# Four PSUM banks for the picks of a graph layer, with a pair's sums moved into the bank of the position row

## The chip, the cores and the metric

The kernel runs on one core of a Trainium2 chip. The metric is the device time of one execution in microseconds (us). The core has TensorE (PE; its weight loads are listed apart as PEld), VectorE (DVE), ScalarE (ACT), GpSimd (POOL) and SyncE (SP, which here only issues DMAs). TensorE writes its products to PSUM, eight banks of 512 32-bit numbers in each of 128 partitions; DVE and ACT read and write PSUM too. Each engine works through its own queue in order, and engines wait for each other through semaphores.

## The reference: what is computed

One message-passing layer on a graph of 6250 nodes and 100000 edges, feature width 128. The edges are sorted by `dst`.

```python
edge_index = jnp.stack([src, dst])          # row = src, col = dst
msg_in = jnp.concatenate([x[row], x[col], edge_attr], axis=-1)
h = msg_in @ W + b                          # (100000, 384) @ (384, 128)
h = (h - mean(h)) * rsqrt(var(h) + 1e-5) * gamma + beta
msg = relu(h)
out = segment_sum(msg, row, num_segments=6250)
x = layernorm(x + out)
```

## The kernel before, in words

The product with `W` is split in three. The part of `x[col]` comes from a table of projected nodes: edges are sorted by `dst`, so the rows that 512 edges need lie in a window of 42 nodes, and a one-hot matrix picks them. The part of the edge's own features is a plain product. Both are added in PSUM for a group of four tiles of 128 edges. There are 782 tiles, 196 such groups, called q. In `edges` TensorE makes them (lines 619 and 623, tile `hp`), in `evict` ACT copies them out (line 633), and in `scatters` POOL writes every row by an indirect DMA to the place in memory that belongs to the block of its `src` (line 650).

That place is computed by `places`, in 20 pieces of 12 to 44 tiles. 50 blocks of 125 nodes hold the sources. A piece makes a one-hot array of blocks by tiles (DVE, line 451, which compares with the position row), scans it for running counts (line 455, which reads a zero beside that row), sums counts over partitions with two small matmuls (lines 467 and 468), adds them to what is already taken (lines 470 to 472), multiplies (line 474), and adds the resulting terms over the 50 blocks (line 502): `PG` blocks side by side in PSUM per matmul, all matmuls adding to the same columns, and DVE adds the `PG` parts in the end (line 507). The pieces are spread over the edge groups by `steps_at`: eleven steps a piece.

The edges are cut in six splits (`SPLITS`). When the rows of one split have arrived, they are loaded back, two blocks at a time: a pair holds eight tiles of rows in splits 0 to 2, six in split 3, four in splits 4 and 5. 25 pairs make a split. The `Pair` class works on the first five splits while later edges are still made; `Unit` works on the last split, in the tail. For a pair:

- `ones`: DVE compares each row's position in its block with the position row (line 742) and so makes one-hot tiles;
- `turn`, `turned`: TensorE transposes them (line 754, bank `tr`), ACT copies them out (line 758);
- `seed`: ACT copies the edge rows into a PSUM bank named `sel` (line 764), up to four tiles to a bank;
- `pick`: TensorE adds to it the rows of `x[row]`'s projection (line 781);
- `square`, `root`, `scale`: ACT sums the squares (lines 790 and 793), DVE makes the reciprocal and scales and clips (lines 799 and 805), which frees the bank;
- `sums`: TensorE adds the messages of each node (line 814, into bank `pa`);
- `add`: DVE adds that to the running total (line 819).

In `Unit` the same steps stand at lines 847 (`ones`), 866 and 872 (`pick`), 883 (`square`), 898 (`scale`), 912 (`sums`, every other one into `pa`, the rest into `hp`) and 918 (`add`); lines 925 to 961 finish the layer norm, and line 930 reads a row of `beta` from the columns of the counts.

The order on PE, DVE, ACT and SP is written out by hand. `work` goes through steps; a pair starts one every four steps, and `FLOW` gives how many steps after its start each part of it is issued:

```python
FLOW = [(14, second(lambda x: x.add())), (11, second(lambda x: (x.root(1), x.scale(1)))),
        (13, single(lambda x: x.add())),
        (9, lambda x: (x.root(0), x.scale(0))), (13, second(lambda x: x.sums())),
        ...
        (10, single(lambda x: x.sums())),
        (0, lambda x: x.ones()),
```

`second` is for pairs with two groups of tiles (eight or six), `single` for pairs of four. So `ones` of pair p+3 is issued at step 12 of pair p, its `sums` at step 13 and its `add` at step 14; for pairs of four `sums` come at step 10, `ones` of pair p+3 at 12 and `add` at 13. `steps_due` ties steps to edge groups. POOL's scatters from group 13 on are tied to TensorE instructions as well, to be spread evenly.

The eight banks are: two `hp`, three `sel`, one `tr`, one `pa`, and one, `beside_t`, with the position row (128 32-bit numbers, `iota_p`), a zero (`zero_p`), 50 numbers of `places` (`at`) and, from column 192, the `counts`. `project`, which makes the tables of projected nodes at the beginning, borrows `sel` and `tr` in turn (lines 391 to 417).

Of the kernel before, what the change touches and what calls it, by code (L numbers as in the profile page):

```python
# [8 lines left out]
F32 = mybir.dt.float32  # L9
BF16 = mybir.dt.bfloat16  # L10
# [6 lines left out]
P = 128  # L17
D = 128
# [6 lines left out]
NB, BN = 50, 125  # L25
# [6 lines left out]
PIECES = 196  # L32
TABLE_FROM = [0, 13, 45, PIECES]
HALF = PIECES // 2
BANKS = {"hp": 2, "sel": 3, "tr": 1}


SPLITS = [(168, 4, 320, [12, 24, 44, 44, 44]),
# [7 lines left out]
BY_PE = 4  # L46
FN = 4

PG = 7
PG_AT = 192  # L50
XG = 4
ROW = 132
ACW = 130
# [13 lines left out]
def dram_ap(t, offset, ap):  # L67
    return bass.AP(tensor=t.tensor, offset=t.offset + offset, ap=ap)
# [7 lines left out]
def row_bc(t, n):  # L76

    return t.unsqueeze(1).to_broadcast([t.shape[0], n, t.shape[1]])


def flat(t):
    return t.rearrange("p t d -> p (t d)")


def fast_path(ctx, tc, io, bad_d, found):
# [3 lines left out]
    nc = tc.nc  # L89
    first_tile = first_tiles()  # L90
    const = ctx.enter_context(tc.tile_pool(name="const", bufs=1))
    dram = ctx.enter_context(tc.tile_pool(name="dram", bufs=1, space=bass.MemoryType.DRAM))
    psum = ctx.enter_context(tc.tile_pool(name="psum", bufs=1, space=bass.MemoryType.PSUM))
# [5 lines left out]
    def pe(i, cost=1):  # L99
        done.append((i.ins, cost))  # L100
        return i
# [72 lines left out]
    iota_i = const.tile([P, P], I32, name="iota_i")  # L174
# [9 lines left out]
    iota_row = const.tile([P, P], F32, name="iota_row")  # L184

    beside_t = psum.tile([P, 512], F32, name="beside")
    beside, counts = beside_t[:, :PG_AT], beside_t[:, PG_AT:]
    iota_p, zero_p, at = beside[:, 0:P], beside[:, P:P + 1], beside[:, P + 8:P + 8 + NB]
    part = const.tile([P, 1], F32, name="part")
    before = const.tile([P, P], BF16, name="before")  # L190
    ident_h = const.tile([P, P], BF16, name="ident_h")
# [7 lines left out]
    over_w = const.tile([P, 2], F32, name="over_w")  # L199

    def constants():
        nc.vector.tensor_copy(iota_p, iota_i)
        nc.vector.tensor_copy(iota_row, iota_i)
        nc.vector.tensor_copy(part, part_i)
        nc.vector.memset(zero_p, 0.0)
        nc.vector.tensor_scalar(over_w[:, 0:1], part, WN - 0.5, float(WN), op0=ALU.is_gt,
                                op1=ALU.mult)
        nc.vector.tensor_scalar(over_w[:, 1:2], part, 2 * WN - 0.5, float(WN), op0=ALU.is_gt,
                                op1=ALU.mult)
        nc.vector.tensor_scalar(before, iota_row, part, None, op0=ALU.is_gt)  # L210
        nc.vector.tensor_tensor(part_w, part, over_w[:, 0:1], op=ALU.subtract)
        nc.vector.tensor_tensor(part_w, part_w, over_w[:, 1:2], op=ALU.subtract)
        nc.vector.tensor_copy(ident_h, ident)
        nc.vector.tensor_scalar(minus_h, ident, -1.0, None, op0=ALU.mult)
# [36 lines left out]
    def signs():  # L251
        nc.vector.tensor_scalar(gamma_r, gamma_r, 0.0, 2.0, op0=ALU.is_ge, op1=ALU.mult)
        nc.vector.tensor_scalar(sgn_r, gamma_r, -1.0, None, op0=ALU.add)
        spread = psum.tile([P, 512], F32, name="pa")[:, :D]
        nc.tensor.matmul(spread, ones_h[0:1, :], sgn_r, start=True, stop=True)
        nc.scalar.copy(sgn, spread)

# [115 lines left out]
    n_banks = 0  # L373

    def store_part(xb_t, i):
        nc.sync.dma_start(dram_ap(xb_d[0], i * TABLES[0][1] * D, [[XG * D, P], [1, XG * D]]),
                          flat(xb_t[:, i]))

    def project(g, k):

        nonlocal n_banks
        t0 = g * XG
        m = XG if k == 1 else min(XG, NB - t0)
        xT = xT_of[g, k % 2]
        name = ("sel", "sel", "tr", "sel")[n_banks % 4]
        n_banks += 1
        ps = psum.tile([P, XG, P], F32, name=name, bufs=BANKS[name])
        for j in range(m):  # L390
            nc.tensor.matmul(ps[:, j, :], xT[:, j * P:(j + 1) * P], w[:, min(k, 1), :],
                             start=j == 0, stop=j == m - 1, skip_group_check=True)
        yield
        full = ps[:, :m, :]
        if k == 0:
            o = [xa[:, t0:t0 + m, i * D:(i + 1) * D] for i in range(3)]
            nc.vector.tensor_tensor(full, full, row_bc(bias, m), op=ALU.add)
            yield
        else:
            xb_t = proj_pool.tile([P, 3, XG, D], BF16, name="xb", bufs=4)  # L400
            o = [xb_t[:, i, :m, :] for i in range(3)]
        for i in range(2):
            nc.scalar.copy(o[i], full)
            if g == 0 and k == 1:
                store_part(xb_t, i)
            yield
            nc.tensor.matmul(full, minus_h, o[i], start=False, stop=True, skip_group_check=True)
            yield
        if g == 0 and k == 1:
            nc.scalar.copy(o[2], full)  # L410
            store_part(xb_t, 2)
            yield
            nc.sync.dma_start(
                dram_ap(xb_d[1], 0, [[XG * D, P], [TABLES[1][1] * D, 3], [1, XG * D]]),
                xb_t.rearrange("p i t d -> p i (t d)"))
            return
        nc.vector.tensor_copy(o[2], full)
        yield
        if k == 1:
            n0 = g * XG * P  # L420
            for (lo, hi), t in zip(TABLES[:2], xb_d):
                if lo <= n0 < hi:
                    nc.sync.dma_start(
                        dram_ap(t, (n0 - lo) * D, [[XG * D, P], [(hi - lo) * D, 3], [1, XG * D]]),
                        xb_t.rearrange("p i t d -> p i (t d)"))
        if k == 2:
            nc.sync.dma_start(
                dram_ap(xb_d[2], t0 * D, [[NB * D, P], [NPAD * D, 3], [1, m * D]]),
                xb_t[:, :, :m, :].rearrange("p i t d -> p i (t d)"))
        yield  # L430
# [7 lines left out]
    def places(s, t0, T):  # L438
# [49 lines left out]
        else:  # L488
# [7 lines left out]
            for k, (wt, v, back) in enumerate(terms):  # L496
                for b in range(0, NB, PG):
                    c0, c1 = b * T, min(b + PG, NB) * T
                    skip = back if b == 0 else 0
# [3 lines left out]
                                     start=(k == 0 and b == 0),  # L503
                                     stop=(k == len(terms) - 1 and b + PG >= NB),
                                     skip_group_check=True)
            yield
            nc.vector.tensor_reduce(pos, sums[:, :PG * T].rearrange("p (g t) -> p t g", g=PG),
                                    axis=AX.X, op=ALU.add)
# [88 lines left out]
    def edge_hot(q):  # L597
# [5 lines left out]
        if q < BY_PE:  # L603
            db = psum.tile([P, PT * P], F32, name="sel", bufs=BANKS["sel"])
            nc.tensor.matmul(db, ones_h[0:1, :], drel0[0:1, q, :], start=True, stop=True)
# [60 lines left out]
    def open_late():  # L666
# [8 lines left out]

        for _ in range(BANKS["sel"]):
            sel = psum.tile([P, PT, P], F32, name="sel", bufs=BANKS["sel"])
            nc.tensor.matmul(flat(sel), ones_h, row_bc(ones_h, PT), start=True, stop=True)
# [29 lines left out]
    def acc_scale(i0, i1):  # L708
        if i0 == 0:
            nc.vector.memset(acc[:, :, D:ACW], 0.0)  # L710
            late["rg"] = psum.tile([P, PT, P], F32, name="sel", bufs=BANKS["sel"])[:, 0, :]
            nc.vector.tensor_copy(late["rg"], rg)
# [15 lines left out]
    class Pair:  # L728
# [17 lines left out]
        def turn(self):  # L746
# [3 lines left out]
            for j0, m in [(0, self.k)]:  # L750
                tr = psum.tile([P, PT, P], F32, name="tr", bufs=BANKS["tr"]).bitcast(BF16)
                tr = tr.rearrange("p t (h d) -> p (t h) d", h=2)
# [54 lines left out]

        def sums(self):
            k = self.k
            pa_t = psum.tile([P, 512], F32, name="pa")  # L810
            self.pa = pa_t[:, :2 * ACW].rearrange("p (h d) -> p h d", h=2)
            for h in range(2):
                for j in range(h, k, 2):
                    pe(nc.tensor.matmul(self.pa[:, h, :], self.ohe[:, j, :], self.msg[:, j, :],  # L814
                                        start=(j == h), stop=(j == k - 2 + h)), 4)
# [12 lines left out]
    class Unit:  # L828
# [73 lines left out]
        def sums(self, g):  # L902
            if (self.p0 + g) % 2:
                pa_t = psum.tile([P, PT, P], F32, name="hp", bufs=BANKS["hp"])
                pa = flat(pa_t)
            else:
                pa = psum.tile([P, 512], F32, name="pa")
            pa = pa[:, :2 * ACW].rearrange("p (h d) -> p h d", h=2)
            for h in range(2):
                for j in range(h, self.kp, 2):  # L910
                    jj = g * self.kp + j
                    nc.tensor.matmul(pa[:, h, :], self.ohe[:, jj, :], self.msg[:, jj, :],
                                     start=(j == h), stop=(j == self.kp - 2 + h))
            self.pa = {**getattr(self, "pa", {}), g: pa}
# [75 lines left out]

    warm_up(6)
    constants()
    signs()
    warm_up(4)
    source_blocks(0, n0, 0)
# [244 lines left out]
    a, b, c, d = units[-4:]  # L1240
# [272 lines left out]
```

## Time and profile before

| | |
|---|---|
| median of 3 runs | 1356.2 us (1353.18 to 1357.1) |
| profiled execution | 1355.95 us, span 1354.1 us |
| mean TensorE clock granted | 0.855 of full speed |
| busy PE, PEld | 978.5, 869.8 us |
| busy DVE, ACT, POOL | 852.2, 766.6, 799.0 us |
| instructions | 27281 |
| mean DMA rate | 183 GB/s |

A group row of the profile names line, engine and operation, what is written and read with its shape, and how often; then the busy time in us, the mean of one in ns, and the idle time of the engine just before, with whoever ended it. "issue" means that the engine waited for nothing the profile shows, "remote" that the source is not told. A row of waits gives who waited for whom, the total in us, how often, and the longest. A timeline row gives start and length in us; consecutive instructions of one kind are merged. Matmuls overlap: a burst's pace is read from the start of one row to the start of the next. An fp32 product counts as two matmuls.

### The profile page before, as it was taken

What the parts mean: (1) busy time and instruction counts of PE and PEld (TensorE: products, weight loads), DVE (VectorE), ACT (ScalarE), POOL (GpSimd) and SP (SyncE); (2) the same over time, 40 slices, a digit from 0 to 9 for tenths busy, and PEclk for the clock granted to TensorE, in tenths of its full rate; (3) what the DMA queues carried; (4) which work ended last, traced back from release to release, by engine and by line L of the source; (5) the groups of instructions that cost most, each with busy time, mean ns of one, the idle gap of its engine ahead of it and who ended that gap; (6) DMA issues with size and microseconds to landing.
All of it is one profiled execution on the core that took longest, in us unless ns stands there. A gap on an engine that the chain in (4) does not pass through costs nothing. (4 is left out here: it accounts for less than half of the span.)

```text
span 1354.1 us, 27281 instructions
## 1 busy us (share of the span) xinstructions
PE 978.5 (72%) x8886; PEld 869.8 (64%) x8886; DVE 852.2 (63%) x2376; ACT 766.6 (57%) x2988; POOL 799.0 (59%) x830
## 2 busy tenths in 40 slices
PE   7555546365768777777877778778878787776895
PEld 5454535344757766676666767777778787665674
DVE  8572425514665666656575667678688877654797
ACT  4223322112656655565555567677779788755796
POOL 3656666666666665666566666656665556556054
PEclk9768687666888887888888798989999999988998
DMA  7857677445666654556756555666667655543332
GB/s 225 251 172 243 191 229 223 138 155 167 192 204 208 203 160 162 166 181 193 219 177 195 174 191 180 218 199 191 188 200 235 189 186 188 158 147 99 108 126 70
DMA packets 128050, 247.20 MB, mean 183 GB/s; under 512 B 47005, under 2 KB 61231, under 8 KB 127897
## 3 DMA queue, kind: packets, MB, share of 16 engines
q1 hardware_dynamic: 101924, 191.92, 46.8%
q0 software_dynamic: 25104, 53.05, 11.1%
q8 instruction: 71, 1.16, 0.4%
q14 instruction: 81, 0.66, 0.1%
q10 hardware_dynamic: 870, 0.40, 0.1%
HBM read 155.49 MB, written 89.80 MB: 181 GB/s over the span
## 5 line engine op out<-in xcount | busy, mean ns | idle before, releaser
L650 POOL DMA_INDIRECT sorted<-hs,place_i x782 | 760.6, 973 | 474.7 <-issue 179.7
L781 PE MATMUL sel<-xa,ohn 128*128 128x128 bf16 x2550 | 210.8, 232 | 134.7 <-issue 65.5
L790 ACT ACTIVATE sq<-sel 128x128 f32<-128x128 f32 x850 | 224.5, 281 | 140.4 <-remote 47.2
L619 PE MATMUL hp<-w,eT 128*128 128x128 f32 x1564 | 261.2, 316 | 32.4 <-issue 20.5
L814 PE MATMUL pa<-msg,ohe 128*128 128x130 f32 x1700 | 259.0, 307 | 30.0 <-DVE msg L805 14.9
L619 PEld LDWEIGHTS hp<-w,eT 128*128 128x128 f32 x1564 | 235.0, 226 | 67.2 <-issue 32.9
L781 PEld LDWEIGHTS <-ohn 128*128 128x128 bf16 x2550 | 175.0, 104 | 154.4 <-issue 136.1
L633 ACT COPY hs<-hp 128x512 f32<-128x512 f32 x196 | 114.2, 584 | 273.9 <-remote 98.5
L814 PEld LDWEIGHTS pa<-msg,ohe 128*128 128x128 f32 x1700 | 234.8, 216 | 41.5 <-issue 24.2
L805 DVE SCALAR_TENSOR_TENSOR msg<-sel,rstd,cut 128x128 f32<-128x128 f32 x850 | 240.7, 346 | 8.0
L790 ACT ACTIVATION_READ_ACCUMULATOR sq<-sel 128x1 f32 x850 | 179.8, 212 | 0.0
L819 DVE TENSOR_TENSOR acc<-acc,pa 128x260 f32<-128x260 f32 x125 | 52.9, 423 | 184.7 <-remote 72.8
L742 DVE TENSOR_TENSOR ohe<-hl,beside 128x1024 f32<-128x1024 f32 (+2 forms) x125 | 131.6, 1053 | 24.2 <-remote 7.6
L758 ACT COPY ohn<-tr 128x1024 bf16<-128x1024 bf16 (+2 forms) x125 | 109.6, 877 | 42.8 <-remote 19.2
L764 ACT COPY sel<-hl 128x512 f32<-128x512 f32 (+1 forms) x225 | 128.5, 571 | 2.0 <-DVE msg L805 2.0
L607 DVE TENSOR_SCALAR ohd<-db,part_w 128x512 bf16<-128x512 bf16 x192 | 68.6, 357 | 68.4 <-remote 36.8
L623 PE MATMUL hp<-win,ohd 126*128 126x128 bf16 x782 | 90.5, 238 | 15.9 <-issue 13.3
L799 DVE RECIPROCAL rstd<-std 128x4 f32<-128x4 f32 (+1 forms) x225 | 38.7, 172 | 90.3 <-ACT std L793 45.2
L754 PE MATMUL tr<-ident_h,ohe 128*128 128x128 bf16 x850 | 77.0, 229 | 21.9 <-issue 19.9
L623 PEld LDWEIGHTS <-ohd 126*128 126x128 bf16 x782 | 69.5, 109 | 23.3 <-issue 18.9
L754 PEld LDWEIGHTS <-ohe 128*128 128x128 bf16 x850 | 57.7, 103 | 29.9 <-issue 29.9
L793 ACT ACTIVATE std<-ss,eps 128x4 f32<-128x4 f32 (+1 forms) x225 | 67.1, 298 | 7.3
(198 smaller groups left out, 1018.9 us busy)
## 6 DMA issues: line engine op xcount, KB each, us to landing
eT<-in_eT SPq DMA_DIRECT2D x96, 512.0 KB
hl<-sorted SPq DMA_DIRECT2D x75, 528.0 KB
db<-drel_d SPq DMA_DIRECT2D x96, 256.0 KB
sorted<-empty SPq DMA_DIRECT2D x100, 198.0 KB
hl<-sorted SPq DMA_DIRECT2D x50, 264.0 KB
sorted<-hs,place_i POOLq DMA_INDIRECT x782
hl<-sorted SPq DMA_DIRECT2D x25, 396.0 KB
sorted<-empty SPq DMA_DIRECT2D x50, 132.0 KB
```

Of the source, the lines that this page charges most:

```text
L619: pe(nc.tensor.matmul(hp[:, j, :], eT[:, at], w[:, 2, :], start=j == 0, stop=False, skip_group_check=True), 4)
L623: pe(nc.tensor.matmul(hp[:, j, :], oh[:3 * WN, at], win[:3 * WN, :], start=False, stop=j == m - 1, skip_group_check=True))
L633: nc.scalar.copy(hs[:, :m, 0:D], hp[:, :m, :])
L650: i = nc.gpsimd.indirect_dma_start(out=sorted_d[s][:, :], out_offset=bass.IndirectOffsetOnAxis(ap=place_i[:parts, t:t + 1], axis=0), in_=h ...
L742: nc.vector.tensor_tensor(self.ohe[:, :k, :], self.hl[:, :k, D:D + 1].to_broadcast([P, k, P]), row_bc(iota_p, k), op=ALU.is_equal)
L754: pe(nc.tensor.transpose(tr[:, j, :], half[:, j0 + j, 1::2], ident_h))
L758: nc.scalar.copy(self.ohn[:, :self.k, :], self.tr[:, :self.k, :])
L764: nc.scalar.copy(self.sel[g][:, :m, :], self.hl[:, j0:j0 + m, 0:D])
L781: pe(nc.tensor.matmul(sel[:, j, :], self.ohn[:, j0 + j, :], xa[:, b, i * D:(i + 1) * D], start=False, stop=j == m - 1 and i == 2, skip_gro ...
L790: nc.scalar.activation(sq[:, j, :], self.sel[g][:, j, :], AF.Square, accum_out=ss[:, j:j + 1])
L805: nc.vector.scalar_tensor_tensor(self.msg[:, j0 + j, 0:D], self.sel[g][:, j, :], rstd[:, j:j + 1], cut, op0=ALU.mult, op1=ALU.max)
L814: pe(nc.tensor.matmul(self.pa[:, h, :], self.ohe[:, j, :], self.msg[:, j, :], start=(j == h), stop=(j == k - 2 + h)), 4)
```

## The change

`sel` gets a fourth bank. The bank `pa` is given up for it, and the sums of a pair (260 columns) move into `beside_t`. To make room there, the position row is kept as 128 16-bit numbers in 64 columns, and the counts get 132 columns in place of 320, so `PG` is 3 in place of 7. `project` goes through five banks in turn in place of four.

```diff
-BANKS = {"hp": 2, "sel": 3, "tr": 1}
+BANKS = {"hp": 2, "sel": 4, "tr": 1}
...
-PG = 7
-PG_AT = 192
+PG = 3
+PG_AT = 120
+PA_AT = 252
...
     beside_t = psum.tile([P, 512], F32, name="beside")
-    beside, counts = beside_t[:, :PG_AT], beside_t[:, PG_AT:]
-    iota_p, zero_p, at = beside[:, 0:P], beside[:, P:P + 1], beside[:, P + 8:P + 8 + NB]
+    counts, sums_p = beside_t[:, PG_AT:PA_AT], beside_t[:, PA_AT:]
+    iota_w, zero_p, at = beside_t[:, 0:P // 2], beside_t[:, P // 2:P // 2 + 1], beside_t[:, 68:68 + NB]
+    iota_p = iota_w.bitcast(BF16)
+    iota_h = const.tile([P, P], BF16, name="iota_h")
...
     def constants():
-        nc.vector.tensor_copy(iota_p, iota_i)
+        nc.vector.tensor_copy(iota_h, iota_i)
+        nc.vector.tensor_copy(iota_w, iota_h.bitcast(F32))
...
     def signs():
...
-        spread = psum.tile([P, 512], F32, name="pa")[:, :D]
+        spread = sums_p[:, :D]
...
-        name = ("sel", "sel", "tr", "sel")[n_banks % 4]
+        name = ("sel", "sel", "tr", "sel", "sel")[n_banks % 5]
...
         def sums(self):
             k = self.k
-            pa_t = psum.tile([P, 512], F32, name="pa")
-            self.pa = pa_t[:, :2 * ACW].rearrange("p (h d) -> p h d", h=2)
+            self.pa = sums_p.rearrange("p (h d) -> p h d", h=2)
...
             else:
-                pa = psum.tile([P, 512], F32, name="pa")
+                pa = sums_p
             pa = pa[:, :2 * ACW].rearrange("p (h d) -> p h d", h=2)
```

## The prediction

> **What bounds the kernel now.** I read the page first, then busy time by stage, then what TensorE (PE) waited for.
>
> ```profile
> span 1354.1 us, 27281 instructions
> PE 978.5 (72%) x8886; PEld 869.8 (64%) x8886; DVE 852.2 (63%) x2376; ACT 766.6 (57%) x2988; POOL 799.0 (59%) x830
> ...
> 345.00:1008.00 663.00, 512.05 (x4912) 465.09 (x4912) 432.91 (x1151) 412.07 (x1621) 409.87 (x422) 0.88 0.61 191
> 1038.00:1107.00 69.00, 57.05 (x632) 54.58 (x630) 55.62 (x160) 57.67 (x242) 39.96 (x42) 0.95 0.59 187
> 1164.00:1244.00 80.00, 59.12 (x575) 54.70 (x576) 44.37 (x139) 50.27 (x214) 43.69 (x46) 0.89 0.44 133
> 1272.00:1354.00 82.00, 67.25 (x624) 51.07 (x622) 71.19 (x289) 64.87 (x332) 36.30 (x35) 0.94 0.29 98
> ```
>
> A stage row gives the stretch, its length, busy us of PE, PEld, DVE, ACT and POOL, then TensorE's clock. The longest stage, 345 to 1008 us, holds pairs of eight tiles; 1038 to 1107 pairs of six; 1164 to 1244 pairs of four; the tail follows. No engine is full, so TensorE's idle time in the long stage must tell who sets the pace:
>
> ```profile
> PE sel L781 <- issue: 52.6, 78, 2.8
> PE sel L781 <- ACT sel L764: 22.7, 19, 3.2
> PE tr L754 <- issue: 16.7, 23, 1.2
> PE beside L502 <- issue: 13.2, 21, 1.2
> PE pa L814 <- issue: 12.7, 24, 1.2
> PE sel L781 <- ACT sc L477: 8.2, 5, 2.4
> PE hp L623 <- issue: 7.3, 13, 1.3
> PE hp L619 <- issue: 5.7, 15, 0.6
> ```
>
> The "issue" rows add to 108.2 us: TensorE stood and waited for nothing the profile shows. With 512 us of work that is 620 of 663 us; the rest is waits for other engines, mostly the two ACT rows here. So TensorE's queue sets the pace, and a new wait in it costs time unless it falls where the queue would have stood anyway. In the tail DVE is fullest (71.19 of 82).
>
> **The change, part by part.**
>
> *A fourth bank for picks.* A bank is taken by ACT's seed copy, which must wait until DVE's scale has freed it.
>
> ```profile
> L764 ACT COPY sel<-hl 128x512 f32<-128x512 f32 (+1 forms) x225 | 128.5, 571 | 2.0 <-DVE msg L805 2.0
> L391 PE MATMUL sel<-w,xT 128*128 128x128 f32 x168 | 30.6, 333 | 4.9 <-issue 3.9 <-DVE oh L451 1.0
> L866 PE MATMUL sel<-hl,ident 128*128 128x512 f32 x38 | 20.0, 608 | 0.0
> ```
>
> All 225 seeds together waited 2.0 us for a bank. The projection, which now rotates over five banks, not four, waited 1.0 us for DVE; the tail's picks waited for nothing. That picks wait for seeds (22.7 us above) comes from ACT's written order, which stays. So a gain of 0 to 3 us; I take 2.
>
> *Narrower position sums (PG 7 to 3).* Of 20 pieces of the placement the first has no such sums, the second two terms, the other 18 three. A term covers its 50 blocks in 17 matmuls, not 8: (18 × 3 + 2) × 9 = 504 more matmuls, each with a weight load, over the same columns.
>
> ```profile
> 733.72 1.01 PE L502 MATMUL beside<-far,twice_f 128*128 128x280 f16 x8
> 734.58 2.03 PE L814 MATMUL pa<-msg,ohe 128*128 128x130 f32 x16
> 738.73 0.83 PE L781 MATMUL sel<-xa,ohn 128*128 128x128 bf16 x12
> 739.40 1.11 PE L619 MATMUL hp<-w,eT 128*128 128x128 f32 x8
> ...
> L502 PEld LDWEIGHTS <-ident_f 128*128 128x128 f16 x160 | 17.1, 111 | 31.0 <-issue 25.9
> ...
> PE beside L502 <- issue: 15.7, 24, 1.2
> ```
>
> From start to start, eight of these matmuls took 0.86 us for 50 × 40 = 2000 columns, 0.43 ns a column; twelve picks of 128 columns took 0.67 us, 56 ns each, of which 55 are columns. So short matmuls with a load each add about 1 ns: 0.5 us in all. At the other end each load overlaps nothing: 504 × 0.111 = 56 us. The picks are the nearest row, so I take 2 us; more matmuls on the same columns cannot gain. Standing for issue came to 15.7 us over the 448 such matmuls of now, 35 ns each; if it goes by count the new ones bring 504 × 0.035 = 18 us, if by time nothing. I take 4, since the stalls are uneven and no row ties them to the count.
>
> The DVE reduction that reads them shrinks:
>
> ```profile
> L507 DVE TENSOR_REDUCE pos<-beside 128x44 f32<-128x308 f32 x3 | 1.4, 473 | 9.2 <-remote 9.2
> L507 DVE TENSOR_REDUCE pos<-beside 128x39 f32<-128x273 f32 x2 | 0.9, 438 | 0.0
> ```
>
> 35 elements are 35 ns, so 168 fewer (of 294) save 0.17 us, 18 times: 3.0 us of DVE, hidden in DVE's idle third; at most 3 us of gain. I take none.
>
> *The position row in 16 bits.* One more cast at the start, of the sort that takes 0.2 us, ahead of a DVE wait:
>
> ```profile
> 1.35 0.28 DVE L202 CAST beside<-iota_i 128x128 f32<-128x128 int32 x1
> 3.92 0.21 DVE L252 TENSOR_SCALAR gamma_r<-gamma_r 1x128 f32<-1x128 f32 x1 [1.14 <-DMA gamma_r<-in_gamma]
> ```
>
> The 1.14 us wait for gamma hides it: nothing. The comparisons that read the row keep their element counts; what a faster rate would bring is a rival below.
>
> *A pair's sums move into the bank of that row.* This is the part that counts. The row is read by DVE's one-hot comparison (line 742) 125 times; the same bank serves nearly every DVE step of the placement. Does sharing cost a wait?
>
> ```profile
> L742 DVE TENSOR_TENSOR ohe<-hl,beside 128x1024 f32<-128x1024 f32 (+2 forms) x125 | 131.6, 1053 | 24.2 <-remote 7.6 <-PE beside L502 6.0 <-PE pa L814 5.7
> L502 PE MATMUL beside<-sc,ident_f 128*128 128x294 f16 (+7 forms) x152 | 25.2, 314 | 4.2 <-issue 3.6 <-DVE ohe L742 0.6
> L814 PE MATMUL pa<-msg,ohe 128*128 128x130 f32 x1700 | 259.0, 307 | 30.0 <-DVE msg L805 14.9 <-issue 14.6
> ```
>
> The comparison reads only the row, L502 writes only the counts beside it, other columns; still the one waited 6.0 us for the other and the other 0.6 us for the one. So columns do not matter, the bank or tile does. The sums (L814) wait for no such reader now; afterwards each must wait for the last DVE step on the bank that the program puts ahead of it, and DVE's next step on it must wait until the sums are done. Behind held sums stand the next edge products, picks and transposes in TensorE's queue; ACT's evictions and copies, and through them POOL's scatters, wait for those. [...]
>
> For the size I put the program's order beside the trace: the comparison of pair p+3 stands one step ahead of the sums of pair p. In 66 of 125 pairs the sums began before the last DVE step on the bank ahead of them had ended; the first and the last of these are
>
> ```profile
> 384.33 1.19 DVE L742 TENSOR_TENSOR ohe<-hl,beside 128x1024 f32<-128x1024 f32 x1
> 385.03 2.00 PE L814 MATMUL pa<-msg,ohe 128*128 128x130 f32 x16
> ...
> 1160.64 0.68 DVE L742 TENSOR_TENSOR ohe<-hl,beside 128x512 f32<-128x512 f32 x1
> 1159.79 1.89 PE L814 MATMUL pa<-msg,ohe 128*128 128x130 f32 x12
> ```
>
> which would wait 0.5 and 1.5 us; the 66 add to 102 us. That is the upper end, paid only if no wait shortens the next. The lower end is 0: a sum held once comes later against DVE, so the next finds the bank free. Between them:
>
> ```profile
> 345.00:1008.00 663.00, 42.68 (x284) 0.00 (x0) 195.52 (x176) 0.88 0.61 191
> 1038.00:1107.00 69.00, 2.94 (x26) 0.00 (x0) 22.31 (x24) 0.95 0.59 187
> ...
> L455 DVE TENSOR_TENSOR_SCAN sc<-oh,sc,beside 128x1050 f16<-128x1050 bf16 x8 | 19.2, 2394 | 0.0
> ```
>
> The first two rows count work on this bank alone (PE, PEld, DVE): DVE holds it 29% and 32% of the time. Sums that arrive at a random moment find it held so often, with half of a step of 1.2 us (comparison) to 2.4 us (scan) left, say 0.8 us: 0.30 × 0.8 = 0.24 us, for 100 pairs 24 us. Half of it should fall on issue stalls or waits for ACT. I take 10 us: nearer to 0 than to 102, since DVE is a third idle and can run ahead.
>
> DVE waits in turn: in 45 places its next step on the bank began before the sums ended, 49 us together, 22 of them comparisons in the pairs of four tiles. There all engines have slack (44.37 of 80 for DVE), so I price it at 0, with 0.68 us × 25 = 17 us if each comparison lands on the chain from sums to add to scale. In the tail every other sum uses the bank, behind a comparison of 1.2 us that runs during the sums ahead of it: nothing, 2 us at most.
>
> **Sum.** −2 + 2 + 4 + 10 = +14 us against the profiled execution's own 1355.95 us (the median is 1356.2, the span 1354.1): 1370 us.
>
> **The rivals.**
>
> *Each wait is paid in full.* If TensorE and DVE stay in step, a held sum delays the square, scale and comparison behind it and the next is held again: 1356 + 102 + 4 = 1462 us, or half of that excess, 1409. For it: 620 of 663 us of TensorE's queue are taken. Against: DVE's idle third.
>
> *The waits are absorbed.* Every held sum falls where TensorE would have stood (108 us of issue in the long stage): 1356 − 2 + 2 = 1356 us, no change. That waits go by columns after all (1360 us) belongs here; the 6.0 us speak against it.
>
> *Faster: the one-hot comparison of the placement doubles its rate.* With row and keys both in 16 bits, line 451 might run like line 480:
>
> ```profile
> L451 DVE TENSOR_TENSOR oh<-bkt_h,beside 128x1200 bf16<-128x1200 bf16 x1 | 1.4, 1394 | 0.0
> L480 DVE TENSOR_TENSOR sc<-sc,oh 128x1200 f16<-128x1200 f16 x1 | 0.8, 776 | 0.0
> ```
>
> That halves 38 steps, 38 × 0.55 = 21 us of DVE. It turns into time only if DVE holds TensorE: with a quarter of it, 2 for the seeds and 3 for the reduction, 1356 − 10 = 1346 us. It decides from the point where sums wait less than 5 us in all. Against: the row is read with one element repeated over all tiles of a block, which line 480 does not do. [...]
>
> *Weight loads bare.* If the loads do not overlap in these bursts, 56 + 18 + 10 us: 1440 us.
>
> **How the numbers follow.** Chances: forecast 0.52 (its own range 1360 to 1390), absorbed 0.20, faster 0.10, waits in full or half 0.12, bare loads 0.06. A measurement of this kernel can tell about 0.3%, 4 us, from no change. Faster: the rival and a little of the absorbed case, 0.12. Same: 0.19, most of the absorbed case and the forecast's foot. Slower: the rest, 0.69. The range leaves out the faster rival's better half and what lies past half-paid waits: 1351 to 1405 us.
>
> **What would show it.** Seeds (L764) no longer wait for DVE. L502 counts 952, L507 shrinks to about 0.29 us; L451 stays near 1.24 us. The sums (L814) get idle time put down to line 742, 451, 455 or 474, some 20 us or more in total, and comparisons get idle time from L814 in the pairs of four tiles. TensorE's issue total grows little. Wrong would be: sums without such waits (columns decide), waits over 60 us that all stay in the span, or a term of L502 far longer than the 0.86 us that one takes now.

## The result and the profile after

The changed kernel took 1414.57 us (median of 6 runs, 1410.46 to 1423.76) where the kernel before took 1357.29 us: 1.0442 times as long, 95% interval 1.0418 to 1.0465. That is 57 us more; 14 more were predicted. The direction was right, the size was not, and the time lies above the range (1351 to 1405 us).

First the page of the changed kernel and its busy time by stage (stretch, length, busy us of PE, PEld, DVE, ACT, POOL, TensorE's clock, DMA share, GB/s). The stages hold the same work as those shown of before: pairs of eight, six and four tiles, then the tail.

```profile
span 1408.7 us, 28285 instructions
PE 980.3 (70%) x9391; PEld 892.9 (63%) x9391; DVE 851.1 (60%) x2377; ACT 765.7 (54%) x2988; POOL 796.1 (57%) x830
...
353.00:1043.00 690.00, 505.89 (x5179) 475.94 (x5177) 432.99 (x1153) 411.39 (x1622) 407.00 (x421) 0.88 0.59 183
1073.00:1148.00 75.00, 56.74 (x617) 53.60 (x618) 53.33 (x153) 55.05 (x230) 37.73 (x40) 0.93 0.54 168
1209.00:1290.00 81.00, 61.79 (x578) 55.95 (x578) 44.18 (x137) 49.72 (x212) 45.19 (x48) 0.89 0.43 133
1319.00:1409.00 90.00, 69.03 (x624) 52.50 (x622) 71.70 (x289) 64.03 (x332) 36.25 (x35) 0.95 0.27 87
```

Busy time is what it was (PE 978.5, DVE 852.2 before), and so is the clock in the long stage. The 54.6 us of added span are engines that stand. The stages grew by 27, 6, 1 and 8 us: the pairs of four tiles, with slack on every engine, lost next to nothing. The rest came between the stages shown and ahead of the first, where 5.0 us were lost before the first pair was added.

Next the groups of the changed kernel whose lines the prediction spoke of (its line numbers are 3 or 4 higher: 742 is 746, 814 is 817, 819 is 822, 764 is 768, 502 is 506, 451 is 455).

```profile
L817 PE MATMUL beside<-msg,ohe 128*128 128x130 f32 x1700 | 276.3, 323 | 115.8 <-issue 45.4 <-DVE ohe L746 34.1 <-DVE far L478 14.0
L746 DVE TENSOR_TENSOR ohe<-hl,beside 128x1024 f32<-128x1024 f32 (+2 forms) x125 | 131.6, 1053 | 63.3 <-PE beside L817 21.2 <-PE beside L506 14.6 <-remote 11.2
L822 DVE TENSOR_TENSOR acc<-acc,beside 128x260 f32<-128x260 f32 x125 | 52.6, 421 | 159.2 <-PE beside L817 83.5 <-PE beside L506 40.2 <-issue 17.4
L768 ACT COPY sel<-hl 128x512 f32<-128x512 f32 (+1 forms) x225 | 128.3, 570 | 0.0
L455 DVE TENSOR_TENSOR oh<-bkt_h,beside 128x1050 bf16<-128x1050 bf16 (+5 forms) x38 | 46.1, 1218 | 19.9 <-remote 11.1 <-PE tr L758 5.1 <-PE sel L785 3.7
L511 DVE TENSOR_REDUCE pos<-beside 128x42 f32<-128x126 f32 (+4 forms) x19 | 5.3, 277 | 30.8 <-remote 18.3 <-PE beside L506 11.4 <-PE sel L785 1.1
L506 PE MATMUL beside<-far,twice_f 128*128 128x126 f16 (+7 forms) x306 | 27.7, 251 | 12.8 <-issue 12.8
```

The sums now stand 115.8 us (30.0 before), behind the comparison of the pairs and behind steps of the placement, DVE's steps on the same bank. The seeds wait for nothing any more. The placement's comparison still takes 1218 ns (1219 before).

What TensorE waited for in the long stage (who waited for whom, total us, times, longest):

```profile
PE beside L817 <- issue: 40.6, 19, 5.5
PE beside L506 <- issue: 26.3, 35, 1.8
PE sel L785 <- issue: 24.4, 37, 1.3
PE beside L817 <- DVE ohe L746: 17.7, 15, 2.7
PE sel L785 <- ACT sel L768: 16.0, 9, 3.7
PE beside L817 <- DVE far L478: 10.0, 4, 4.3
```

The first row was 12.7 us before, 1.2 us at most at a time, and what is new in it is not what it is called. A timeline (start, length) of two places with such "issue":

```profile
646.34 1.22 DVE L746 TENSOR_TENSOR ohe<-hl,beside 128x1024 f32<-128x1024 f32 x1
647.47 2.40 DVE L459 TENSOR_TENSOR_SCAN sc<-oh,sc,beside 128x1050 f16<-128x1050 bf16 x1
649.92 1.45 PE L817 MATMUL beside<-msg,ohe 128*128 128x130 f32 x5 [3.88 <-issue]
...
701.67 1.21 DVE L746 TENSOR_TENSOR ohe<-hl,beside 128x1024 f32<-128x1024 f32 x1
702.80 1.19 DVE L455 TENSOR_TENSOR oh<-bkt_h,beside 128x1000 bf16<-128x1000 bf16 x1
704.05 0.80 PE L817 MATMUL beside<-msg,ohe 128*128 128x130 f32 x2 [4.63 <-issue]
```

The sums start 0.05 and 0.06 us after a DVE step on their bank has ended, and behind the comparison DVE runs a second step on that bank at once. These are waits for the shared bank that the profile could not put down to anyone. So I counted from the trace every first product of a pair's sums that started over 0.3 us after the product before it, and took the gap as held by the bank if one of the four DVE steps on the bank had ended at most 0.25 us earlier:

```
kernel                     held sums  us held   by: pairs' comparison, scan, placement's comparison, its product
before                         0        0.0
changed                       58      104.3      56.7   10.4   16.7   20.5
changed, long stage alone     37       78.9      35.6   10.4   15.5   17.3
```

The weight load of each of the 58 products waits for a semaphore that DVE's steps raise (sums wait there for their messages too). In 57 of them, those at 649.92 and 704.05 us included, the DVE step that had just ended is one that raises it. So the program holds the sums there until DVE's last step on the bank is over. The shared bank is also one tile of the program in every run; whether bank or tile sets this order, the runs cannot tell.

The upper end of the prediction, 102 us over 66 sums, is what was paid at the sums themselves. Not all of it reaches the end: in the long stage 79 us are held and the stage is 27 us longer, with the added matmuls in it. Part of the difference shows in the rows above: picks stood 52.6 us for issue before and stand 24.4 us now, and their waits for seeds fell from 22.7 to 16.0 us.

### The profile page after: what moved, and what is told of

The parts are those of the page before. It is cut to its first block, busy times and chain, and to the rows that moved or that the text cites. A ratio compares the mean times of both kernels' runs of the same rounds, so it can differ in the third digit from the quotient of the medians.

```text
span 1408.7 us, 28285 instructions
## 1 busy us (share of the span) xinstructions
PE 980.3 (70%) x9391; PEld 892.9 (63%) x9391; DVE 851.1 (60%) x2377; ACT 765.7 (54%) x2988; POOL 796.1 (57%) x830
## 5 line engine op out<-in xcount | busy, mean ns | idle before, releaser
L817 PE MATMUL beside<-msg,ohe 128*128 128x130 f32 x1700 | 276.3, 323 | 115.8 <-issue 45.4
L817 PEld LDWEIGHTS beside<-msg,ohe 128*128 128x128 f32 x1700 | 248.6, 229 | 134.8 <-issue 50.9
L623 PE MATMUL hp<-w,eT 128*128 128x128 f32 x1564 | 248.8, 308 | 40.4 <-issue 34.3
L623 PEld LDWEIGHTS hp<-w,eT 128*128 128x128 f32 x1564 | 226.7, 219 | 60.4 <-issue 48.4
L785 PE MATMUL sel<-xa,ohn 128*128 128x128 bf16 x2550 | 200.0, 229 | 81.7 <-ACT sel L768 42.7
L785 PEld LDWEIGHTS <-ohn 128*128 128x128 bf16 x2550 | 171.2, 103 | 96.5 <-issue 73.5
L746 DVE TENSOR_TENSOR ohe<-hl,beside 128x1024 f32<-128x1024 f32 (+2 forms) x125 | 131.6, 1053 | 63.3 <-PE beside L817 21.2
L822 DVE TENSOR_TENSOR acc<-acc,beside 128x260 f32<-128x260 f32 x125 | 52.6, 421 | 159.2 <-PE beside L817 83.5
L627 PE MATMUL hp<-win,ohd 126*128 126x128 bf16 x782 | 85.0, 233 | 12.3 <-issue 10.2
```

Of the source, the lines that this page charges most:

```text
L623: pe(nc.tensor.matmul(hp[:, j, :], eT[:, at], w[:, 2, :], start=j == 0, stop=False, skip_group_check=True), 4)
L627: pe(nc.tensor.matmul(hp[:, j, :], oh[:3 * WN, at], win[:3 * WN, :], start=False, stop=j == m - 1, skip_group_check=True))
L746: nc.vector.tensor_tensor(self.ohe[:, :k, :], self.hl[:, :k, D:D + 1].to_broadcast([P, k, P]), row_bc(iota_p, k), op=ALU.is_equal)
L785: pe(nc.tensor.matmul(sel[:, j, :], self.ohn[:, j0 + j, :], xa[:, b, i * D:(i + 1) * D], start=False, stop=j == m - 1 and i == 2, skip_gro ...
```

## The experiments

T1: the waits on the shared bank carry most of the 57 us. T2: the 504 added matmuls carry 30 us or more. T3: the fourth bank and the projection's new rotation do harm. The kernel before takes 1356 to 1358 us in some groups of runs and 1373 to 1375 us in others. It is not simply the chip: chip 5 gave 1355.73 us in one group and 1373.14 us in a later one, and the reason is open. Every ratio below is to the kernel before on the same chip in the same group, and 0.1% is 1.4 us.

### Parts of the change, by bank

*Three pick banks.* The changed kernel with the old rotation; the eighth bank stays empty.

```diff
-BANKS = {"hp": 2, "sel": 4, "tr": 1}
+BANKS = {"hp": 2, "sel": 3, "tr": 1}
-        name = ("sel", "sel", "tr", "sel", "sel")[n_banks % 5]
+        name = ("sel", "sel", "tr", "sel")[n_banks % 4]
```

> Three theories for the 57 us. T1: the sums and the DVE steps that now share a bank wait for each other, and this carries 40 us or more. T2: the 504 added matmuls and the standing for issue that comes with them carry 30 us or more. T3: the fourth pick bank and the projection's new rotation do harm. This kernel is the changed one with three pick banks and the old rotation; the freed bank stays empty. T1 and T2: 1410 to 1420 us, as with four. T3: under 1390 us.

Measured 1.0406 (1.0387 to 1.0424). T3 falls; the fourth bank brings nothing that can be told from zero.

*All but the sharing.* The kernel above, with the sums back in a bank of their own.

```diff
-            self.pa = sums_p.rearrange("p (h d) -> p h d", h=2)
+            pa_t = psum.tile([P, 512], F32, name="pa")
+            self.pa = pa_t[:, :2 * ACW].rearrange("p (h d) -> p h d", h=2)
...
-                pa = sums_p
+                pa = psum.tile([P, 512], F32, name="pa")
```

> All of the change but the sharing: 16-bit row, counts with three blocks side by side, three pick banks, and the sums in a bank of their own as before. T1: 1356 to 1368 us (my terms of 2 to 6 us for the added matmuls, and no wait). T2: 1387 us or more. T3: about 1356 us, like T1, so the kernel with three pick banks must tell T1 and T3 apart.

Measured 1.0134 (1.0097 to 1.0171), about 18 us: neither theory's value. A third of the loss has nothing to do with the sharing.

*The sums with the row alone, and with the counts alone.* Three pick banks; a second bank takes the part that the sums don't share.

```diff
+    other_t = psum.tile([P, 512], F32, name="other_bank")
-    counts, sums_p = beside_t[:, PG_AT:PA_AT], beside_t[:, PA_AT:]
+    counts, sums_p = other_t[:, PG_AT:PA_AT], beside_t[:, PA_AT:]     # row with sums
+    counts, sums_p = other_t[:, PG_AT:PA_AT], other_t[:, PA_AT:]      # counts with sums
```

In both the 50 numbers of the placement go with the counts.

> Three pick banks; the position row and the zero share a bank with the sums, while the counts and the 50 numbers of the placement lie in another bank. The sums then meet the one-hot comparisons of the pairs, those of the placement and the scan, but not the products of the placement. T1: 1385 to 1405 us, because the comparison of the pairs carries most of the named waits of the sums (34 of 75 us put down to DVE), with the scan and the placement's comparison another 13. T2: as the kernel with the own bank, so 1387 or more there too.

> Three pick banks; the counts and the 50 numbers of the placement share a bank with the sums, while the position row and the zero have a bank of their own. The sums then meet only the placement's additions, products and reduction. T1: 1362 to 1380 us, since the placement's products carry 14 of the 75 us of named waits. T2: as the kernel with the own bank. If the two parts of the sharing add, the excess of this kernel and of the one with row and sums together make that of the full change.

Measured 1.032 (1.0275 to 1.0365) with the row and 1.0204 (1.0157 to 1.0251) with the counts. The second lies above T1's 1362 to 1380 us (at most 1.017), which lacked the 18 us just found. Over the kernel with the own bank these are 25.6 and 9.6 us, each uncertain by about 8 us; together 35.2 us, and the full sharing (1.0406) is 37.4 us over it. The two parts add within that. T1 holds, for about two thirds of the loss and a little under its own 40 us.

### What the other third is

*The kernel before, traced in the group of the next two runs.*

> The kernel before, unchanged, for its trace on the chip on which the next kernels run. TensorE busy near 980 us, issue near 108 us in the stage of the pairs of eight tiles, whatever the theory; if the chip of this call is slower, the loss should lie in a lower granted clock.

One time, 1372.27 us, at a clock of 0.856 (0.855 in the first trace): the lower clock that was expected is not there, and why this group is slower stays open.

*Three blocks side by side, nothing else.*

```diff
-PG = 7
+PG = 3
```

> The kernel before with three blocks side by side in place of seven and nothing else: 504 more small matmuls, a reduction of 3 in place of 7. The kernel with the own bank was 1.3% slower than before. If the added matmuls carry that (T2, in part): 1.010 to 1.017 of before, with TensorE's standing at that line up from 16 to 30 us or more. If the 16-bit row carries it: 0.998 to 1.004.

*The 16-bit row, nothing else* (counts of seven blocks from column 120, three pick banks, sums in their own bank).

```diff
-        nc.vector.tensor_copy(iota_p, iota_i)
+        nc.vector.tensor_copy(iota_h, iota_i)
+        nc.vector.tensor_copy(iota_w, iota_h.bitcast(F32))
```

> The kernel before with the position row in 16 bits, seven blocks side by side as before, three pick banks, sums in their own bank. If the added matmuls carried the 1.3% of the kernel with the own bank: 0.997 to 1.004. If the 16-bit row does (some slower read on DVE, or another placement of columns): 1.010 or more, and a one-hot comparison longer than its 1.05 us.

Measured 1.0142 (1.0111 to 1.0173) for the matmuls, 1.0009 (0.9991 to 1.0027) for the row. The 504 matmuls cost 19.5 us, the row nothing. TensorE's standing at that line, first before, then with three blocks:

```profile
PE beside L502 <- issue: 12.1, 17, 1.1
```

```profile
PE beside L502 <- issue: 52.9, 70, 1.9
```

The matmuls themselves cost what was predicted: among the last pieces, where no stall fell, a piece's products took 2.55 us from the first start to the last before and 2.93 us with three blocks, which for 18 pieces is 7 us at most (2.66 and so 2 us in the kernel with the own bank); the middle of all distances from start to start is 58 ns. It is the standing that grew, by 40.8 us.

*More blocks in place of fewer.* The 16-bit row leaves room for nine or ten, with the sums in their own bank; that makes 112 and 168 matmuls fewer than before.

```diff
-PG = 3
+PG = 9      # or 10, with `at` on free columns of the counts
```

> The 16-bit row makes room for nine blocks side by side in the counts (six matmuls a term in place of eight), with three pick banks and the sums in their own bank: 112 matmuls fewer than before. The 504 added ones cost 19.5 us, 39 ns each. If the price goes by count: 4 us less than before, 0.995 to 0.999. If it is the break below some length or a full queue: 0.999 to 1.002.

> As the kernel with nine, but ten blocks side by side (five matmuls a term, 168 fewer than before); the 50 numbers of the placement lie on columns of the counts that are free at that time. By count: 6.5 us less than before, 0.993 to 0.998. The reduction that reads the counts grows by 0.13 us, 18 times, on DVE, which I take as hidden.

Measured 0.9994 (0.9977 to 1.0011) and 0.999 (0.9971 to 1.0008): no gain that can be told. By count, at 39 ns a matmul, 4 and 6.5 us less were due, 0.9968 and 0.9952; both lie outside the intervals. So 39 ns is not a price per matmul; below the old count it is not won back.

*The added matmuls in shorter bursts.* Three blocks side by side in the kernel before, each of a piece's three terms at a place of its own in TensorE's order: 17 matmuls in a row, not 51.

```diff
-            at_slots = [int(free + i * T / 42) for i in (0, 1, 2, 3, 4, 4, 5, 6, 7, 8, 9)]
+            at_slots = [int(free + i * T / 42) for i in (0, 1, 2, 3, 4, 4, 5, 6, 7, 8, 9, 10)]
...
             for k, (wt, v, back) in enumerate(terms):
...
-            yield
+                if not early or k:
+                    yield
```

> The kernel before with three blocks side by side (504 more matmuls), but the three terms of a piece stand at three places of TensorE's order, 17 matmuls each, in place of 51 in a row. In the unsplit kernel the stalls of over 0.4 us come at any place of the burst, mostly after the first 15. If they come from the length of the run of short matmuls: stalls at that line fall from some 60 to under 30 and the time to 1.003 to 1.009 of before. If they go by count: 1.011 to 1.017, as unsplit.

Measured 1.0041 (1.0018 to 1.0065), but with 41 stalls, not under 30, and in another group of runs than the unsplit form. The next three kernels, unsplit, split and the full change, are from one chip and one group:

> The kernel before with three blocks side by side, unsplit, now beside its split form on one chip. If the length of the burst sets the price: 1.010 to 1.017 of before, and 60 or more stalls of over 0.4 us between the placement's products, excess over 50 us. If the unsplit form is as cheap on this chip as the split one was on another: under 1.007, and the reading of the split falls.

> Its split form, 17 matmuls at a place. If the length of the burst sets the price: 1.002 to 1.007 of before, at least 0.5% below the unsplit form. If the lower price on the other chip was the chip's: within 0.2% of the unsplit form.

> The changed kernel beside the two, so that the share of the matmuls and that of the sharing come from one chip: 1.038 to 1.048 of before. If the added matmuls take 1.4%, the sharing takes the other 2.6 to 3.0%, about 38 us; if the unsplit form is cheap here, the sharing takes nearly all.

Measured 1.014 (1.0112 to 1.0167) unsplit, 1.0048 (1.0027 to 1.0069) split, 1.0418 (1.038 to 1.0456) for the full change. Unsplit, then split:

```profile
PE beside L502 <- issue: 54.0, 71, 2.1
```

```profile
PE beside L503 <- issue: 29.7, 46, 1.8
```

The same 952 matmuls cost 19.2 us over the kernel before in bursts of 51 and 6.6 us in bursts of 17. Two thirds of their price goes with the length of the burst, or with the places in TensorE's order that the split gives the terms; no run parts the two. TensorE's clock does not explain it: the unsplit runs with the highest and the lowest clock (0.858 and 0.837) took 1396.78 and 1392.70 us. A burst of the unsplit kernel in the timeline:

```profile
308.96 1.38 PE L502 MATMUL beside<-sc,minus_f 128*128 128x125 f16 x17
310.18 0.57 PE L502 MATMUL beside<-far,twice_f 128*128 128x126 f16 x5
311.27 0.21 PE L502 MATMUL beside<-far,twice_f 128*128 128x126 f16 x1 [0.52 <-issue]
312.00 0.22 PE L502 MATMUL beside<-far,twice_f 128*128 128x126 f16 x1 [0.51 <-issue]
313.40 0.26 PE L502 MATMUL beside<-far,twice_f 128*128 128x126 f16 x1 [1.18 <-issue]
314.12 0.28 PE L502 MATMUL beside<-far,twice_f 128*128 128x126 f16 x1 [0.46 <-issue]
```

It runs 39 matmuls at full pace and then one every 0.7 or 1.4 us. What TensorE's queue lacks at that moment no view shows. Instructions on their way are not it: none of the trace's transfers of instructions starts between 287.3 and 325.6 us, and none takes over 1.7 us. Nor is it a trait of these bursts alone: the picks of the kernel before stood 52.6 us for issue in the long stage, most often with 0.7 us from start to start.

### What in the sharing costs

*The pairs' and the tail's comparison read the row from SBUF* (in 32 bits); the sums then share the bank with the placement alone.

```diff
-                                    row_bc(iota_p, k), op=ALU.is_equal)
+                                    row_bc(iota_row, k), op=ALU.is_equal)
```

> The changed kernel, but the pairs' and the tail's one-hot comparisons read the position row from SBUF as 32-bit numbers; only the placement still reads the row in PSUM. The sums then meet only the placement's steps. T1 with the pairs' comparison as the main reader: 1.015 to 1.025 of before, near the kernel where the counts share with the sums (1.020). If the placement's steps are what hold the sums: 1.035 or more. A comparison that takes longer from SBUF would add 0.1 us times 125 of DVE at most, mostly hidden.

Measured 1.0196 (1.016 to 1.0232), beside 1.0142 for the matmuls alone in the same group of runs. So the sharing with the placement costs 7 us, and the comparison, with 2.2% between this and the full change of the other group (1.0418), 30 us; both are uncertain by 6 to 7 us. By the count used above the sums are still held 59.1 us here, all but 0.3 of it by steps of the placement. Overlaps with these steps alone, counted in the trace of before, come to 58.7 us over 30 sums: the count foretells the held time. But held time and price don't go together: 59 us cost 7 here, and in the full change of the other group 95.4 us cost 38.

*The comparison one step later*, behind the sums.

```diff
-            (0, lambda x: x.ones()),
+            (1, lambda x: x.ones()),
...
-                if off == 0:
+                if off == 1:
```

> The changed kernel with the pairs' one-hot comparison issued one step later, so that it stands behind the sums of the pair three ahead and not in front of them; the tail keeps its order. If the sums are held because the program puts the comparison's read of the bank just ahead of them (T1): 1.022 to 1.030 of before, near the kernel whose comparison reads SBUF (1.020) plus the tail's share. If the comparison then only hands the wait to DVE and on to the transposes and picks, or if it is access to the bank and not the order that costs: 1.036 or more.

Measured 1.0628 (1.0592 to 1.0663), the worst of all. What TensorE and DVE waited for in it:

```profile
PE tr L758 <- DVE ohe L746: 73.9, 51, 4.5
PE beside L817 <- issue: 26.4, 21, 4.2
...
DVE ohe L746 <- PE beside L817: 97.9, 48, 8.0
```

The sums no longer wait for the comparison. The comparison waits for the sums instead (21.2 us in the changed kernel), and the transposes, a step behind it in TensorE's order, wait for the comparison.

*The comparison one step earlier.*

```diff
-            (0, lambda x: x.ones()),
+            (-1, lambda x: x.ones()),
...
-                if off == 0:
+                if off == -1:
```

> The changed kernel with the pairs' one-hot comparison issued one step earlier: two steps ahead of the sums of the pair three before it, where the changed kernel has one step and the kernel with the later comparison has it behind them. If the sums are held because the comparison stands just ahead of them and runs late: sums waiting for the comparison fall from 34 us to under 10 and the time to 1.020 to 1.032 of before. If any order of the two on one bank costs the same, since TensorE and DVE follow each other in step: 1.038 or more, with the wait named at another place (the comparison waiting for the sums of the pair before, as in the kernel with the later comparison).

Measured 1.0461 (1.0432 to 1.049), the same as the change within the intervals. What TensorE waited for:

```profile
PE beside L817 <- issue: 44.4, 26, 5.1
PE beside L817 <- DVE ohe L746: 21.0, 17, 3.8
PE beside L817 <- DVE far L478: 16.9, 10, 3.3
PE beside L817 <- DVE sc L459: 15.2, 6, 5.1
```

Neither expectation came out whole. The named waits for the comparison fell, to 21 us and not under 10, and by the count above from 56.7 to 24.7 us. But the placement's steps took their place, 47.6 before, 74.4 now, so that the sums are held 99.1 us, nearly as long as in the changed kernel. A later reader took over the wait, and the time stayed. The comparison's own wait for the sums did not grow (22.0 us).

*Ten blocks and terms at three places, without the sharing.* Ten blocks side by side, sums in their own bank, three pick banks, the terms at three places.

> The kernel with ten blocks side by side (0.999 of before) with its three terms at three places of TensorE's order, five matmuls each. Its stalls of over 0.4 us at that line held 4.8 us in all, so the split can bring 5 us at most: 0.995 to 1.000.

Measured 0.9975 (0.9952 to 0.9997), 3.4 us less than before, at the edge of what can be told. It keeps the 16-bit row and drops the rest of the change. The changed kernel with split terms was not tried; there a pair's sums would fall between two terms that add up in the same bank.

## Why the prediction was wrong in size

In the group that holds unsplit, split and full change, where the kernel before takes 1373 us, the full change is 57.4 us. The matmuls are 19 of it, the sharing 38. Of the 38 the placement's steps against the sums are 7 (from the kernel that reads SBUF, in another group), which leaves the comparison against the sums 31, of which 7.5 in the tail. Term by term:

- *Seeds, −2:* their waits went (2.0 to 0.0 us), the time did not. Three and four banks can't be told apart (1.0406 and 1.0442, or 1.0418 in the later group).
- *504 matmuls, +2:* right. 58 ns from start to start, as the nearest row (picks, 56 ns) said. The rival with bare loads falls with it.
- *Issue, +4 with 18 as the upper end:* mis-sized. TensorE's standing at that line went from 15.7 to 34.9 us in the two profiles first shown, 36.7 ns a matmul, so the price by count that I had written down and then not taken fits there; in the group of the unsplit form's first run it grew by 40.8 us, over twice its bound. My reason was "no row ties them to the count". What I did not ask is whether they go by the length of a burst, which the change doubles, from 24 to 51 matmuls a piece. Of this term and the one above, 19 us reached the end.
- *Reduction 0, row 0:* right. The reduction takes 0.28 us, the 16-bit row alone 1.0009. The rival in which line 451 doubles its rate falls: 1218 ns a step with the row in 16 bits, 1219 in 32. Whether the element repeated over the tiles of a block is the reason, as the prediction argued, no run shows.
- *Sums waiting for the bank, +10:* the step that failed. Waits do not go by columns, as the 6.0 us of before showed and the 104 us show again: the sums have columns that none of these DVE steps touches. But I took sums to arrive at a random moment of DVE's work, 24 us, and halved it. They don't: a sum becomes ready when DVE's scale has made its messages, and the next things in DVE's own queue are the comparison and the placement's step. At 649.92 us the sums waited 3.88 us for two such steps one behind the other. So the overlaps counted in the trace of before, 66 sums and 102 us, were no upper end but the measure of the held time: 58 sums, 104 us. What reached the end outside the tail is some 30 us, where the term had 10.
- *"A third of DVE is idle and can run ahead":* wrong here. DVE reads what TensorE's sums free and TensorE waits for what DVE scales; with one bank between them every order of comparison and sums left the kernel at 1.042 or more. The rival "half of the excess, 1409 us" came nearest, but by luck: it gave the bank 51 us and all the rest 2, and the bank cost 38 and the matmuls 19.
- *DVE's waits in turn, 0:* right for the pairs of four tiles. From the add of pair 99 to that of pair 124 it is 107.8 us before and 109.9 us now.
- *Tail, 0, at most 2:* mis-sized, it is 7.5 us. From the start of the last pair's add to the end of the last computing instruction it is 76.9 us before, 84.4 us in the changed kernel, and 76.9 us where the comparison reads SBUF. The row, of the changed kernel:

```profile
L915 PE MATMUL beside<-msg,ohe 128*128 128x130 f32 x104 | 15.3, 288 | 6.2 <-DVE ohe L850 6.1
```

I had the comparison running "during the sums ahead of it"; it ran during the sums on its own bank, and in the tail DVE is the fullest engine (71.70 of 90 us).

What the runs leave open: what makes TensorE stand in a long burst; why 59 us of held sums cost 7 us and the 36 us that the comparison adds cost 30. That the comparison also stands in front of the transposes and of DVE's scale is argued from the kernel with the later comparison, not shown.

## What to carry to other kernels

Before two engines are given one PSUM bank, count in the trace how often one's steps overlap the other's in program order, and take that total as the held time: here 102 us were counted and 104 held, where the prediction's estimate for meeting at random was 24. It is not the price; of 95 us held 38 reached the end, of 59 us 7. In both other orders tried here (1.0628 and 1.0461) the wait was paid elsewhere while the bank stayed shared; a reader taken off the bank (1.0196) or sums put in their own (1.0134) is what removed it. The 504 added short matmuls cost 19.2 us in bursts of 51 and 6.6 us in bursts of 17 at other places of TensorE's order, so spread such matmuls.

## What was not expected of the hardware

- In bursts of 51 short matmuls with a load each, TensorE stopped, mostly with 0.7 or 1.4 us from the start of one matmul to that of the next, 71 times in one run, 66 of them after twenty or more matmuls of the burst, with nothing that the profile shows to wait for. In bursts of 17 it did so 46 times, and with ten blocks (15 longer matmuls a burst) 7 times.
- "Issue" in front of an instruction that touches a shared bank can be a wait for that bank's last user: in 353 to 1043 us the sums' 40.6 us of issue and 39.5 us named for DVE add to 80.1, and 78.9 us of that ended within 0.25 us after a DVE step on the bank.
- Reading the position row from SBUF left the comparison as fast as from PSUM (1055 and 1053 ns), but POOL's scatters grew from 969 ns to 1019 ns, 39 us of POOL in all; in every other trace they take 968 to 973 ns. The rows of the changed kernel, then of the kernel that reads SBUF:

```profile
L654 POOL DMA_INDIRECT sorted<-hs,place_i x782 | 757.8, 969 | 521.0 <-issue 181.6 <-PE beside L817 112.0 <-PE sel L785 60.2
```

```profile
L746 DVE TENSOR_TENSOR ohe<-hl,iota_row 128x1024 f32<-128x1024 f32 (+2 forms) x125 | 131.9, 1055 | 0.0
L654 POOL DMA_INDIRECT sorted<-hs,place_i x782 | 797.1, 1019 | 482.2 <-issue 183.8 <-PE beside L817 89.7 <-PE sel L785 50.0
```

The edit changes only where the comparisons, 147 us in all, read the row; how that reaches the scatters no run shows. POOL stands 482 us ahead of these steps, and nothing here shows that it cost time.
